# A depthwise 7x7 convolution as band products: blocks of four rows by 32 columns in place of two rows by 64

## The chip, the cores and the metric

The kernel runs on one core of a Trainium2 chip. The metric is the device time of one execution in microseconds. The engines are PE (TensorE, matrix products; PEld is its weight load), DVE (VectorE), ACT (ScalarE), POOL (GpSimd) and SP (SyncE, which only issues transfers here). All transfers of the core are carried by the same 16 DMA engines.

## The reference

Four layers act on x, eight images of 56 x 56 pixels and 192 channels in fp32. Each takes a group normalisation of x, computes something, and adds it to x. Layer 0 is a Toeplitz mixing network, layer 1 windowed attention, layer 2 a projection with a 3x3 depthwise convolution, running averages in four directions and a second projection. The change is in layer 3:

```python
x = x + _L3_conv_ref(_gn(x), ...)
# in _L3_conv_ref:
y = lax.conv_general_dilated(x, dw_kernel, window_strides=(1, 1), padding='SAME',
                             feature_group_count=c, ...) + dw_bias   # 7x7, each channel alone
y = (y - mu) * lax.rsqrt(var + EPS) * ln_gamma + ln_beta             # over the 192 channels
y = gelu(y @ w0 + b0)                                                # 192 -> 768
return (y @ w1 + b1) * gamma                                         # 768 -> 192
```

## The kernel before

**Layout.** Most of the kernel holds channels on partitions: 64 channels at a time for the upper and lower half of an image, thus 128 partitions, and three such thirds. For the depthwise convolution of layer 3 this is turned round: pixels lie on partitions and channels on the free axis, so that a 7x7 filter of one channel is a product with a band matrix.

**Preparing the images (`layer3_in`, L1190).** It runs image by image inside the loop of layer 2's output, as a generator that is advanced between the steps of that loop. It takes the group statistics, scales the image into `zp` (L1207, POOL; rows padded to 64 columns, one row of zeros above and below), and for each third of the channels turns pairs of rows into columns: 15 transposes on PE into `zps` (L1222), each 2 rows x 64 columns = 128 pixels, then copies on ACT into `zt` (L1230, and two short ones at L1233 and L1234, where the halves of the image meet). POOL fills the ends of `zt` with zeros (L1215, L1216). SP writes `zt` to the HBM buffer `zd[b]` (L1235). `NB` = 31 pairs of rows are kept per channel.

**The convolution (`convolve`, L1237).** It takes the channels in 12 groups of 16, all eight images at once. For each group SP loads the band matrices `wt` (L1250) and the images `zc` (L1253, one transfer an image), and PE computes for each channel four products into one PSUM region (L1262): `wt[:, c, q*128:(q+1)*128]` with the row pairs `q` to `q + 27` of all images, q = 0 to 3, 224 columns each. A pair of output rows needs the rows of four pairs of input rows, hence four. The band matrices are not stored: HBM holds 640 numbers a channel, and the transfer reads them with a step of one number from partition to partition, so that each partition gets 512 numbers (2 KB) a channel. DVE and ACT copy the results to `yc` (L1272, L1274), SP writes them to `yd[b]` (L1276), and POOL fetches image 0 from there at once (L1277) and adds the bias (L1286). `wt`, `zc` and `yc` have two buffers each, the PSUM tile three. SP issues in a fixed order: weights of group g+2, eight results of group g, eight images of group g+2, weights of g+3. A weight load waits until PE has ended the group whose buffer it takes. Transfers of SP share eight completion counters in turn, so each waits for the one eight places ahead: the last of the eight results waits for the weights to land, and the last of the images for the last of the results.

**After it (`layer3_norm`, L1293, and `layer3_out`).** Statistics over the channels, two per pixel pair; scaling on DVE into `yt` (L1317), transposes back on PE (L1338), and an activation with gain and shift on ACT into `y` (L1349), four pairs of rows at a time; then the two matrix products (L1361, L1372), PE's main work to the end. `layer3_norm` is a generator too, advanced inside `layer3_out`.

**The order of the work.** Within `convolve` and `layer3_in` a scheduler sets the order of instructions by its own costs, except where `manual_schedule` keeps the program's order (DVE in the loop of layer 2's output; PE, ACT and DVE in the last loop).

Of the kernel before, what the change touches and what calls it, by code (L numbers as in the profile page):

```python
# [45 lines left out]


NPAIR = H // 2
NB = NPAIR + 3
WS = 64  # L50
QR = 56 * 64
OP = 2 * WS
BAND = 4 * OP
BL = BAND + OP
CG = 16

P2 = NPAIR + 1
# [34 lines left out]
def kernel(ctx: ExitStack, tc: tile.TileContext, a: dict, out: bass.AP):  # L92
# [107 lines left out]
    def ln_var(st, nch, pool):  # L200


        P, _, n, _ = st.shape
        new = lambda name: pool.tile([P, 2, PH], F32, name=name)[:, :, 0:n]

        mean, d, var = new("ln_mean"), new("ln_d"), new("ln_var")
        nc.vector.tensor_tensor(mean, st[:, :, :, 1], st[:, :, :, 4], ALU.add)
        nc.vector.tensor_tensor(d, st[:, :, :, 1], st[:, :, :, 4], ALU.subtract)
        nc.vector.tensor_tensor(d, d, d, ALU.mult)
        nc.vector.tensor_tensor(var, st[:, :, :, 2], st[:, :, :, 5], ALU.add)  # L210
        nc.vector.tensor_scalar(var, var, 1.0 / nch, None, ALU.mult)
        nc.vector.scalar_tensor_tensor(var, d, 0.25, var, ALU.mult, ALU.add)
        return mean, var

    def ln_rows(mean, var, eps, pool):

        P, _, n = var.shape
        new = lambda name: pool.tile([P, 2, PH], F32, name=name)[:, :, 0:n]
# [4 lines left out]
        return rs, mr  # L223

    def in_halves(st):
        return st.rearrange("p (s n) k -> p s n k", s=2)
# [960 lines left out]
        nc.vector.scalar_tensor_tensor(xs, ps[:, 0:nt], vec("b_out", j), xs, ALU.add, ALU.add)  # L1187


    def layer3_in(b, x, zp, pool, psum):  # L1190
# [12 lines left out]
        yield  # L1203
        run(finish)

        for j in range(3):
            nc.gpsimd.tensor_scalar(  # L1207
                zp[:, j, 1:H // 2 + 1, 0:W], x[:, j].rearrange("p (h w) -> p h w", w=W),
                sc, sh, ALU.mult, ALU.add,
            )  # L1210
        yield

        for j in range(3):
            zt = pool.tile([OP, 64, NB], F32, name="zt")
            nc.gpsimd.memset(zt[:, :, 0:1], 0.0)  # L1215
            nc.gpsimd.memset(zt[:, :, NB - 1:NB], 0.0)  # L1216
            for m0 in range(0, PH + 1, 4):
                yield
                tp = psum.tile([OP, 4, 2, 64], F32, name="zps")
                nm = min(4, PH + 1 - m0)  # L1220
                for i in range(nm):
                    nc.tensor.transpose(  # L1222
                        tp[:, i].rearrange("p s c -> p (s c)"),
                        zp[:, j, 2 * (m0 + i):2 * (m0 + i) + 2].rearrange("p h w -> p (h w)"), ident,
                    )

                n2 = min(nm, PH - m0)
                dst = zt[:, :, 1 + m0:1 + m0 + n2]
                dst = bass.AP(dst.tensor, dst.offset, [list(dst.ap[0]), [1, n2], [PH, 2], [NB, 64]])
                nc.scalar.copy(dst, tp[:, 0:n2])  # L1230
                if nm > n2:

                    nc.scalar.copy(zt[:, :, 1 + 2 * PH], tp[:, n2, 1])  # L1233
                    nc.scalar.copy(zt[0:64, :, 1 + PH], tp[0:64, n2, 0])  # L1234
            nc.sync.dma_start(zd[b][:, 64 * j:64 * j + 64], zt)  # L1235

    def convolve(first, dwb):  # L1237
# [3 lines left out]
        with ExitStack() as st:  # L1241
            pool = st.enter_context(tc.tile_pool(reuse_waits="tile", name="cv", bufs=2))
            psum = st.enter_context(tc.tile_pool(reuse_waits="tile", name="cvp", bufs=3, space=PSUM))
            for g in range(C // CG):
                cs = slice(g * CG, g * CG + CG)
                wt = pool.tile([OP, CG, BAND], F32, name="wt")
                src = bass.AP(band.tensor, band.offset + g * CG * BL, [[1, OP], [BL, CG], [1, BAND]])

                n, queues = (CG, (nc.sync,)) if g else (4, (nc.sync, nc.gpsimd, nc.scalar))
                nc.sync.dma_start(wt[:, 0:n], src[:, 0:n])  # L1250
# [6 lines left out]
                for c4 in range(0, CG, 4):  # L1257
                    ps = psum.tile([OP, 2, 512], F32, name="cps")
                    for i in range(4):
                        dst = ps[:, i // 2, 256 * (i % 2):256 * (i % 2) + nimg * NPAIR]  # L1260
                        for q in range(4):
                            nc.tensor.matmul(  # L1262
                                dst.rearrange("p (b n) -> p b n", n=NPAIR),
                                wt[:, c4 + i, q * OP:(q + 1) * OP], zc[:, :, c4 + i, q:q + NPAIR],
                                start=(q == 0), stop=(q == 3),
                            )
# [26 lines left out]
    def layer3_norm(yl, pool, psum, dwb):  # L1293
# [7 lines left out]
        if not first:  # L1301
            for n in range(0, NPAIR, 7):
                add_bias(yl[:, :, n:n + 7], dwb)
            for k in range(5):
                yield
                ln_pieces(st, yl, range(NPAIR * k // 5, NPAIR * (k + 1) // 5))
            rows = ln_var(in_halves(st), C, pool)
            yield
            rs, mr = ln_rows(*rows, eps6, pool)

        def scaled(i0):

            yt = pool.tile([OP, 4, 3, 2, 64], F32, name="yt3")
            for i in range(min(4, PH - i0)):
                for s in range(2):
                    k = i if first else i0 + i
                    nc.vector.tensor_scalar(  # L1317
                        yt[:, i, :, s], yl[:, :, PH * s + i0 + i].rearrange("p (j c) -> p j c", j=3),
                        rs[:, s, k:k + 1], mr[:, s, k:k + 1], ALU.mult, ALU.add,
                    )  # L1320
            return yt

        ready = None
        for i0 in range(0, PH + 4, 4):
            yield
            if i0 < PH:
                if first:
                    ns = slice(i0, min(i0 + 4, PH))
                    ln_pieces(st, yl, [PH * s + n for s in range(2) for n in range(ns.start, ns.stop)])
                    rs, mr = ln_rows(*ln_var(in_halves(st)[:, :, ns], C, pool), eps6, pool)  # L1330
                following = scaled(i0)
            if ready is not None:
                i1 = i0 - 4
                ni = min(4, PH - i1)
                for j in range(3):
                    tp = psum.tile([128, 4, OP], F32, name="tp3")
                    for i in range(ni):
                        nc.tensor.transpose(  # L1338
                            tp[:, i], ready[:, i, j].rearrange("p s c -> p (s c)"), ident[0:OP, 0:OP]
                        )  # L1340

                    src = tp[:, 0:ni].rearrange("p i (s w) -> p i s w", s=2)
                    dims = [list(z) for z in src.ap]
                    src = bass.AP(
                        src.tensor, src.offset + OP - 1,
                        [dims[0], dims[1], [-dims[2][0], 2], [-dims[3][0], W]],
                    )
# [219 lines left out]
    with ExitStack() as st:  # L1567
# [6 lines left out]
        zp = pool.tile([128, 3, H // 2 + 2, WS], F32, name="zp", bufs=1)  # L1574
        nc.gpsimd.memset(zp, 0.0)
        x = [load_halves(pool, x2[0], "x2o")]
        if nimg > 1:
            ml.append(layer2_load(1, pool))
# [18 lines left out]
        for n in range(-1, len(groups)):  # L1597
# [26 lines left out]
            if k == 3:  # L1624
                run(steps)
                nc.sync.dma_start(xd[b], x[b])
                steps = layer3_in(b, x[b], zp, pool, psum)
        run(steps)


# [35 lines left out]
def _lay_out(inp):  # L1666
# [101 lines left out]
```

## Time and profile before

| | us |
|---|---|
| median of 3 runs (5647.63 to 5649.4) | 5648.63 |
| the profiled execution | 5648.44 |
| its span | 5646.6 |
| layer 3's convolution, first to last product | 303.3 (4449.5 to 4752.8) |
| PE busy in it | 299.6 |
| DVE, ACT, POOL busy in it | 29.4, 25.0, 16.3 |
| one image in the loop of layer 2's output | 57.9 |
| mean granted PE clock over the span | 0.961 |

Over the whole span PE is busy for 91%, DVE for 54%, ACT for 41%, POOL for 33%. These are averages over layers with different limits, so a stage has to be read by itself. In the profile, L12 is line 12 of the kernel. A row of a group gives the line, engine, operation, tiles and shapes, then the count, the busy time in us and the mean in ns, then the idle time of the engine just before those instructions and what ended it. Buffer numbers are left out of the names, so layer 2's convolution (L1088) and layer 3's (L1262) both show tiles `zc` and `wt`, at different lines; a name such as `in_band_dram` covers the band matrices of both layers.

### The profile page before, as it was taken

What the parts mean: (1) busy time and instruction counts of PE and PEld (TensorE: products, weight loads), DVE (VectorE), ACT (ScalarE), POOL (GpSimd) and SP (SyncE); (2) the same over time, 40 slices, a digit from 0 to 9 for tenths busy, and PEclk for the clock granted to TensorE, in tenths of its full rate; (3) what the DMA queues carried; (4) which work ended last, traced back from release to release, by engine and by line L of the source; (5) the groups of instructions that cost most, each with busy time, mean ns of one, the idle gap of its engine ahead of it and who ended that gap; (6) DMA issues with size and microseconds to landing.
All of it is one profiled execution on the core that took longest, in us unless ns stands there. A gap on an engine that the chain in (4) does not pass through costs nothing. (4 is left out here: it accounts for less than half of the span.)

```text
span 5646.6 us, 113339 instructions
## 1 busy us (share of the span) xinstructions
PE 5131.2 (91%) x49446; PEld 3421.6 (61%) x49446; DVE 3030.6 (54%) x4087; ACT 2287.3 (41%) x3100; POOL 1839.5 (33%) x1583
## 2 busy tenths in 40 slices
PE   7899969999999789999997989998888797999999
PEld 6798866666666445555554756775344697444444
DVE  4565534555554456556665868888787103433331
ACT  3344445555555333333331025554667201333333
POOL 5565655555555233334431023333010101101000
PEclk9999979999999889999998999999999898999999
DMA  5988996777777512223225756676677686212211
GB/s 148 235 226 227 223 299 245 272 273 272 273 273 274 151 36 80 74 73 81 75 62 144 266 213 228 231 241 190 185 205 212 247 330 257 78 59 78 80 39 26
DMA packets 556148, 1013.75 MB, mean 180 GB/s; under 512 B 256104, under 2 KB 479684, under 8 KB 528884
## 3 DMA queue, kind: packets, MB, share of 16 engines
q1 hardware_dynamic: 542896, 956.63, 52.8%
q0 software_dynamic: 8512, 40.62, 2.2%
q10 hardware_dynamic: 4244, 9.26, 0.6%
q8 instruction: 389, 6.37, 0.5%
q14 instruction: 107, 0.88, 0.0%
HBM read 676.92 MB, written 345.97 MB: 181 GB/s over the span
## 5 line engine op out<-in xcount | busy, mean ns | idle before, releaser
L460 POOL COPY lc<-lt 128x896 f32<-128x896 f32 (+1 forms) x320 | 590.3, 1854 | 542.8 <-PE op L468 506.6
L427 PE MATMUL qv<-w_qv_sb,x 64*112 64x256 f32 (+1 forms) x5376 | 685.7, 408 | 16.3 <-DVE act L433 12.4
L427 PEld LDWEIGHTS qv<-w_qv_sb,x 64*112 64x112 f32 x5376 | 600.2, 175 | 90.8 <-DVE act L433 22.6
L433 DVE TENSOR_TENSOR act<-qv,b_qv 112x640 f32<-112x640 f32 x448 | 318.8, 753 | 320.4 <-PE qv L427 245.0
L437 ACT ACTIVATE act<-act 112x640 f32<-112x640 f32 x448 | 300.6, 683 | 413.2 <-DVE act L433 402.7
L403 POOL TENSOR_TENSOR qv<-act 112x320 f32<-112x320 f32 x448 | 346.7, 798 | 288.4 <-ACT act L437 209.4
L468 PE MATMUL op<-rc,lc 128*56 128x56 f32 x9216 | 350.0, 221 | 61.5 <-POOL lc L460 33.0
L468 PEld LDWEIGHTS op<-rc,lc 128*56 128x56 f32 x9216 | 326.3, 135 | 129.5 <-POOL lc L460 56.6
L1361 PE MATMUL ph<-y,w_sb 64*128 64x392 f32 x2304 | 398.2, 498 | 6.5 <-ACT hid L1365 6.5
L1372 PE MATMUL po<-hid,w_sb 128*64 128x392 f32 x2304 | 386.3, 494 | 0.0
L1379 DVE TENSOR_TENSOR x<-x,z 128x392 f32<-128x392 f32 x96 | 69.6, 725 | 523.5 <-ACT z L1377 523.5
L1088 PE MATMUL cv<-zc,wt 128*128 128x224 f32 x1536 | 312.6, 355 | 25.3 <-DMA zc<-pd 24.6
L1088 PEld LDWEIGHTS cv<-zc,wt 128*128 128x128 f32 x1536 | 290.1, 189 | 68.8 <-issue 53.2
L877 PE MATMUL qk_ps<-xr,wg 64*96 64x392 f32 x1536 | 329.8, 531 | 1.7 <-DVE xr L824 1.7
L1361 PEld LDWEIGHTS ph<-y,w_sb 64*128 64x128 f32 x2304 | 220.2, 188 | 176.4 <-issue 26.1
L922 POOL TENSOR_TENSOR e<-e,mx 128x1176 f32<-128x1176 f32 x64 | 140.0, 2188 | 561.6 <-DVE mx L921 534.9
L478 PE MATMUL pj<-xn,w_p_sb 64*128 64x392 f32 x1536 | 288.8, 508 | 32.7 <-ACT pp L485 31.6
L1262 PE MATMUL cps<-zc,wt 128*128 128x224 f32 x1536 | 299.6, 356 | 18.0 <-DMA zc<-zd 15.9
L1103 POOL TENSOR_TENSOR rows<-rows,loc 128x896 f32<-128x896 f32 x96 | 218.8, 2279 | 274.7 <-ACT rows L1099 209.8
L1262 PEld LDWEIGHTS cps<-zc,wt 128*128 128x128 f32 x1536 | 289.6, 189 | 28.1 <-issue 20.5
L501 PE MATMUL y<-pp,w_o_sb 128*64 128x392 f32 x1536 | 301.2, 497 | 0.5 <-DVE pp L495 0.5
L460 DVE COPY rc<-rt 128x896 f32<-128x896 f32 (+1 forms) x160 | 215.3, 1346 | 150.4 <-PE op L468 96.8
(245 smaller groups left out, 8927.3 us busy)
## 6 DMA issues: line engine op xcount, KB each, us to landing
lt<-left SPq DMA_DIRECT2D x72, 1792.0 KB
rt<-right SPq DMA_DIRECT2D x72, 1792.0 KB
left<-qv SPq DMA_DIRECT2D x224, 252.0 KB
right<-qv SPq DMA_DIRECT2D x96, 504.0 KB
wt<-in_band_dram SPq DMA_DIRECT2D x23, 2048.0 KB
wt<-in_band_dram SPq DMA_DIRECT2D x11, 4096.0 KB
zc<-pd SPq DMA_DIRECT2D x187, 232.0 KB
pd<-pt SPq DMA_DIRECT2D x7, 5568.0 KB
```

The source lines that it names most:

```text
L403: nc.gpsimd.tensor_tensor(qv[:, s, s0:s1, k], *(acts[s][:, which, 0:n].rearrange("p (s d) -> p s d", d=64) for which in range(2)), ALU.mult,)
L427: nc.tensor.matmul(ps[s][:, which, 0:n], x[64 * s:64 * s + 64, j, bass.ts(i, 2 * W)], w_qv[64 * s:64 * s + 64, j, which, 64 * s0:64 * s1], ...
L433: nc.vector.tensor_tensor(acts[s][:, :, 0:n], ps[s][:, :, 0:n], b_qv[:, :, 64 * s0:64 * s1], ALU.add)
L437: nc.scalar.activation(acts[s][:, :, 0:n], acts[s][:, :, 0:n], AF.Silu)
L460: copy(c[:, 0:nu], raw.rearrange("p (w u d) -> p u d w", u=nu, d=64 // nu)[:, :, d0:d0 + 8])
L468: nc.tensor.matmul(op[64 * u:64 * u + W, i, :], lc[:, u, i], rc[:, u, i], start=True, stop=True)
L501: nc.tensor.matmul(y[64 * s:64 * s + 64], w_o[:, 2 * g + u, 64 * j:64 * j + 64], pp[:, u, s], start=(u == 0), stop=(u == 1),)
L877: nc.tensor.matmul(in_pairs(ps[s]), wg[64 * s:64 * s + 64, j, c0:c0 + HC], in_slots(xr[64 * s:64 * s + 64], (3 * g + j) * GW), start=(j == ...
L1088: nc.tensor.matmul(dst, wt[:, c4 + i, 128 * q:128 * q + 128], zc[:, :, c4 + i, q:q + NPAIR], start=(q == 0), stop=(q == 1),)
L1262: nc.tensor.matmul(dst.rearrange("p (b n) -> p b n", n=NPAIR), wt[:, c4 + i, q * OP:(q + 1) * OP], zc[:, :, c4 + i, q:q + NPAIR], start=(q ...
L1361: nc.tensor.matmul(ps[:, s, 0:TT], w0[64 * s:64 * s + 64, j, m * 128:(m + 1) * 128], y[64 * s:64 * s + 64, j, ts], start=(j == 0), stop=(j ...
L1372: nc.tensor.matmul(ps[64 * s:64 * s + 64], w1[:, m, 64 * j:64 * j + 64], hid[:, m, s], start=(m == 0), stop=(m == 5),)
```

## The change

The image of layer 3 is cut into a left half and a right half of 31 columns each (columns 0 to 30 and 25 to 55; 28 of each half's results are used), set in rows of 32. A block of pixels on the 128 partitions is then four rows by 32 columns. There are seven blocks in each half of the rows, 14 for each half of the columns, and a zero block at either end: `NB` = 32. Four output rows need the rows of three blocks, so a channel has three products, each still of 224 columns (8 images x 2 halves x 14 blocks). With only one empty column in 32, a band that is shifted from partition to partition would let the end of a row reach into the next, so HBM now holds the band matrices written out, 128 x 192 x 384 numbers (37.7 MB in place of 0.5 MB), and a partition's part of a group lies in one piece of 24 KB.

`layer3_in` scales into `zq` (both column halves, which overlap by six columns), makes 14 transposes and four copies for each third of the channels, and needs no short copies. `layer3_norm` picks 28 columns of each half out of the transposed blocks, and takes the statistics in quarters (row half x column half) in place of halves. The order of the transfers around the products stays as it was; around the transposes of `layer3_in` the scheduler places some transposes and copies differently.

```diff
-NB = NPAIR + 3
-WS = 64
+NQUAD = H // 4
+NB = 2 * (NQUAD + 2)
-OP = 2 * WS
-BAND = 4 * OP
-BL = BAND + OP
+QW = 32
+OP = 4 * QW
...
         for j in range(3):
+            xj = x[:, j]
             nc.gpsimd.tensor_scalar(
-                zp[:, j, 1:H // 2 + 1, 0:W], x[:, j].rearrange("p (h w) -> p h w", w=W),
+                zq[:, j, :, :, 0:QW - 1],
+                bass.AP(xj.tensor, xj.offset, [list(xj.ap[0]), [W - QW + 1, 2], [W, H // 2], [1, QW - 1]]),
                 sc, sh, ALU.mult, ALU.add,
             )
...
             zt = pool.tile([OP, 64, NB], F32, name="zt")
-            nc.gpsimd.memset(zt[:, :, 0:1], 0.0)
-            nc.gpsimd.memset(zt[:, :, NB - 1:NB], 0.0)
-            for m0 in range(0, PH + 1, 4):
-                yield
-                tp = psum.tile([OP, 4, 2, 64], F32, name="zps")
-                nm = min(4, PH + 1 - m0)
-                for i in range(nm):
-                    nc.tensor.transpose(
-                        tp[:, i].rearrange("p s c -> p (s c)"),
-                        zp[:, j, 2 * (m0 + i):2 * (m0 + i) + 2].rearrange("p h w -> p (h w)"), ident,
-                    )
-                n2 = min(nm, PH - m0)
-                dst = zt[:, :, 1 + m0:1 + m0 + n2]
-                dst = bass.AP(dst.tensor, dst.offset, [list(dst.ap[0]), [1, n2], [PH, 2], [NB, 64]])
-                nc.scalar.copy(dst, tp[:, 0:n2])
-                if nm > n2:
-                    nc.scalar.copy(zt[:, :, 1 + 2 * PH], tp[:, n2, 1])
-                    nc.scalar.copy(zt[0:64, :, 1 + PH], tp[0:64, n2, 0])
+            ends = zt.rearrange("p c (h n) -> p c h n", h=2)
+            for n in (0, NQUAD + 1):
+                nc.gpsimd.memset(ends[:, :, :, n], 0.0)
+            for h in range(2):
+                for m0, nm in ((0, 4), (4, 3)):
+                    yield
+                    tp = psum.tile([OP, 4, 2, 64], F32, name="zps")
+                    for i in range(nm):
+                        nc.tensor.transpose(
+                            tp[:, i].rearrange("p s c -> p (s c)"),
+                            zq[:, j, h, 4 * (m0 + i):4 * (m0 + i) + 4].rearrange("p r w -> p (r w)"), ident,
+                        )
+                    dst = ends[:, :, h, 1 + m0:1 + m0 + nm]
+                    dst = bass.AP(dst.tensor, dst.offset, [list(dst.ap[0]), [1, nm], [NQUAD // 2, 2], [NB, 64]])
+                    nc.scalar.copy(dst, tp[:, 0:nm])
             nc.sync.dma_start(zd[b][:, 64 * j:64 * j + 64], zt)
...
-                wt = pool.tile([OP, CG, BAND], F32, name="wt")
-                src = bass.AP(band.tensor, band.offset + g * CG * BL, [[1, OP], [BL, CG], [1, BAND]])
+                wt = pool.tile([OP, CG, 3 * OP], F32, name="wt")
+                src = band[:, cs]
...
-                        for q in range(4):
+                        z = zc[:, :, c4 + i].rearrange("p b (h n) -> p b h n", h=2)
+                        for q in range(3):
                             nc.tensor.matmul(
-                                dst.rearrange("p (b n) -> p b n", n=NPAIR),
-                                wt[:, c4 + i, q * OP:(q + 1) * OP], zc[:, :, c4 + i, q:q + NPAIR],
-                                start=(q == 0), stop=(q == 3),
+                                dst.rearrange("p (b h n) -> p b h n", h=2, n=NQUAD),
+                                wt[:, c4 + i, q * OP:(q + 1) * OP], z[:, :, :, q:q + NQUAD],
+                                start=(q == 0), stop=(q == 2),
                             )
...
-                    src = tp[:, 0:ni].rearrange("p i (s w) -> p i s w", s=2)
-                    dims = [list(z) for z in src.ap]
-                    src = bass.AP(
-                        src.tensor, src.offset + OP - 1,
-                        [dims[0], dims[1], [-dims[2][0], 2], [-dims[3][0], W]],
-                    )
-                    dst = y[:, j, 2 * W * i1:2 * W * (i1 + ni)].rearrange("p (i s w) -> p i s w", s=2, w=W)
+                    part = list(tp.ap[0])
+                    src = bass.AP(tp.tensor, tp.offset, [part, [ni * OP + QW - W // 2 - 1, 2], [QW, 4 * ni], [1, W // 2]])
+                    dst = y[:, j, 4 * W * i1:4 * W * (i1 + ni)].rearrange("p (r h w) -> p h r w", h=2, w=W // 2)
                     nc.scalar.activation(dst, src, AF.Identity, bias=vec("be3", j), scale=vec("g3", j))
...
-    band = np.zeros((C, BL), np.float32)
-    for i in range(7):
-        band[:, 124 + WS * i:131 + WS * i] = l3("dw_kernel")[i, :, 0].T
+    band = np.zeros((4, QW, C, 3, 4, QW), np.float32)
+    for q, r, p, m, dx in np.ndindex(3, 4, 4, QW - 1, 7):
+        dy, c = 4 * (q - 1) + p - r + 3, m + dx - 3
+        if 0 <= dy < 7 and 0 <= c < QW - 1:
+            band[p, c, :, q, r, m] = l3("dw_kernel")[dy, dx, 0]
+    band = band.reshape(OP, C, 3 * OP)
```

More of the change, by code (lines that the diff above doesn't have):

```diff
@@ L200, in ln_var @@
     def ln_var(st, nch, pool):
-        P, _, n, _ = st.shape
-        new = lambda name: pool.tile([P, 2, PH], F32, name=name)[:, :, 0:n]
+        P, A, n, _ = st.shape
+        new = lambda name: pool.tile([P, A, NPAIR // A], F32, name=name)[:, :, 0:n]
         mean, d, var = new("ln_mean"), new("ln_d"), new("ln_var")
@@ L215, in ln_rows @@
     def ln_rows(mean, var, eps, pool):
-        P, _, n = var.shape
-        new = lambda name: pool.tile([P, 2, PH], F32, name=name)[:, :, 0:n]
+        P, A, n = var.shape
+        new = lambda name: pool.tile([P, A, NPAIR // A], F32, name=name)[:, :, 0:n]
         rs, mr = new("ln_rs"), new("ln_mr")
@@ L223, in ln_rows, with in_quarters @@
         return rs, mr
+    def in_quarters(st):
+        return st.rearrange("p (k n) e -> p k n e", k=4)
     def in_halves(st):
@@ L1187, in layer2_out, with layer3_in @@
         nc.vector.scalar_tensor_tensor(xs, ps[:, 0:nt], vec("b_out", j), xs, ALU.add, ALU.add)
-    def layer3_in(b, x, zp, pool, psum):
+    def layer3_in(b, x, zq, pool, psum):
         sc = pool.tile([128, 1], F32, name="sc3")
@@ L1306, in layer3_norm @@
                 ln_pieces(st, yl, range(NPAIR * k // 5, NPAIR * (k + 1) // 5))
-            rows = ln_var(in_halves(st), C, pool)
+            rows = ln_var(in_quarters(st), C, pool)
             yield
             rs, mr = ln_rows(*rows, eps6, pool)
+        NQ = NQUAD // 2
         def scaled(i0):
             yt = pool.tile([OP, 4, 3, 2, 64], F32, name="yt3")
[L1314 to L1319, printed above, removed]
-                    )
+            ni = min(2, NQ - i0)
+            for h, i, s in np.ndindex(2, ni, 2):
+                k = i if first else i0 + i
+                nc.vector.tensor_scalar(
+                    yt[:, ni * h + i, :, s], yl[:, :, NQUAD * h + NQ * s + i0 + i].rearrange("p (j c) -> p j c", j=3),
+                    rs[:, 2 * h + s, k:k + 1], mr[:, 2 * h + s, k:k + 1], ALU.mult, ALU.add,
+                )
             return yt
         ready = None
-        for i0 in range(0, PH + 4, 4):
+        for i0 in range(0, NQ + 2, 2):
             yield
-            if i0 < PH:
+            if i0 < NQ:
                 if first:
-                    ns = slice(i0, min(i0 + 4, PH))
-                    ln_pieces(st, yl, [PH * s + n for s in range(2) for n in range(ns.start, ns.stop)])
-                    rs, mr = ln_rows(*ln_var(in_halves(st)[:, :, ns], C, pool), eps6, pool)
+                    ns = slice(i0, min(i0 + 2, NQ))
+                    ln_pieces(st, yl, [NQ * k + n for k in range(4) for n in range(ns.start, ns.stop)])
+                    rs, mr = ln_rows(*ln_var(in_quarters(st)[:, :, ns], C, pool), eps6, pool)
                 following = scaled(i0)
             if ready is not None:
-                i1 = i0 - 4
-                ni = min(4, PH - i1)
+                i1 = i0 - 2
+                ni = min(2, NQ - i1)
                 for j in range(3):
                     tp = psum.tile([128, 4, OP], F32, name="tp3")
-                    for i in range(ni):
+                    for i in range(2 * ni):
                         nc.tensor.transpose(
@@ L1340, in layer3_norm @@
                         )
-                    src = tp[:, 0:ni].rearrange("p i (s w) -> p i s w", s=2)
-                    dims = [list(z) for z in src.ap]
-                    src = bass.AP(
-                        src.tensor, src.offset + OP - 1,
-                        [dims[0], dims[1], [-dims[2][0], 2], [-dims[3][0], W]],
-                    )
-                    dst = y[:, j, 2 * W * i1:2 * W * (i1 + ni)].rearrange("p (i s w) -> p i s w", s=2, w=W)
+                    part = list(tp.ap[0])
+                    src = bass.AP(tp.tensor, tp.offset, [part, [ni * OP + QW - W // 2 - 1, 2], [QW, 4 * ni], [1, W // 2]])
+                    dst = y[:, j, 4 * W * i1:4 * W * (i1 + ni)].rearrange("p (r h w) -> p h r w", h=2, w=W // 2)
                     nc.scalar.activation(dst, src, AF.Identity, bias=vec("be3", j), scale=vec("g3", j))
@@ L1573 @@
         w_out = resident("w_out", nc.gpsimd, pool)
-        zp = pool.tile([128, 3, H // 2 + 2, WS], F32, name="zp", bufs=1)
-        nc.gpsimd.memset(zp, 0.0)
+        zq = pool.tile([128, 3, 2, H // 2, QW], F32, name="zq", bufs=1)
+        nc.gpsimd.memset(zq, 0.0)
         x = [load_halves(pool, x2[0], "x2o")]
@@ L1626 @@
                 nc.sync.dma_start(xd[b], x[b])
-                steps = layer3_in(b, x[b], zp, pool, psum)
+                steps = layer3_in(b, x[b], zq, pool, psum)
         run(steps)
```

## The prediction

> **What bounds the kernel now.** I began with the page's list of costly groups, which gives the convolution's row, and then followed the chain that ended last through the stage that the change touches.
>
> ```profile
> L1262 PE MATMUL cps<-zc,wt 128*128 128x224 f32 x1536 | 299.6, 356 | 18.0 <-DMA zc<-zd 15.9
> L1262 PEld LDWEIGHTS cps<-zc,wt 128*128 128x128 f32 x1536 | 289.6, 189 | 28.1 <-issue 20.5
> ```
>
> The 192 channels with four band products each are 768 products, and each leaves two records (fp32), so a group of 16 channels is 128 records. They fill 299.6 us, and of the 18.0 us of idleness before them 15.9 are waits for images, 14.3 of that ahead of the first product.
>
> ```profile
> 4439.51 9.88 DMA zc<-zd
> 4449.39 0.14 issue
> 4449.52 76.31 PE cps L1262 x384
> ...
> 4601.17 14.64 DMA wt<-in_band_dram
> 4615.82 4.58 DMA yd<-yc
> 4620.42 5.69 DMA zc<-zd
> 4626.11 0.35 issue
> 4626.46 24.89 PE cps L1262 x128
> ```
>
> In this chain of work (start, length, what) a group of 128 records takes 24.89 us on PE. The middle lines are the lesson: 4601.17 to 4626.11, the transfers of one group, one behind the other, take 24.94 us. PE and transfers are level. The stages show how much slack the transfers have (columns: window, its length, busy PE, PEld, DVE, ACT, POOL, then granted clock, DMA share, GB/s):
>
> ```profile
> 4449.50:4752.80 303.30, 299.56 (x1536) 289.57 (x1536) 29.37 (x47) 25.02 (x47) 16.31 (x22) 0.99 0.85 310
> 4449.50:4454.00 4.50, 4.48 (x12) 4.08 (x13) 0.00 (x0) 0.00 (x0) 0.00 (x0) 0.51 1.05 396
> 4552.00:4574.00 22.00, 22.00 (x116) 21.48 (x116) 1.88 (x3) 1.64 (x4) 1.48 (x2) 1.00 1.02 375
> 4574.00:4577.00 3.00, 2.19 (x12) 1.83 (x11) 0.62 (x1) 0.53 (x1) 0.00 (x0) 1.00 0.08 29
> 4588.00:4598.50 10.50, 10.50 (x57) 10.26 (x56) 1.25 (x2) 1.06 (x2) 1.48 (x2) 1.00 1.04 395
> 4764.00:4782.00 18.00, 2.84 (x9) 1.59 (x10) 16.65 (x35) 1.39 (x4) 10.33 (x4) 0.50 1.00 428
> ```
>
> The DMA engines are full for 22 us of each group, then empty for 3 us until PE frees a weight buffer. So the stage is PE's, by 3 us in 25. It is 303.3 us = 12 x 24.89 (298.7) + 2.25 (the first 4.5 us run at half clock) + 2.3 of small waits. SP's own waits say the same from the other side:
>
> ```profile
> SPq L1250 <- PE cps L1262: 53.9, 10, 7.0
> SPq L1276 <- DMA wt<-in_band_dram: 51.7, 10, 6.1
> ```
>
> The weight load of a group (L1250) waits for PE; the last write of results (L1276) waits until that load has landed, and the image loads (L1253) stand behind it on SP.
>
> **What the Trainium skill says.** DMA: Bandwidth & Descriptors, "Latency and other measured facts", lists rates that fall when rows of different partitions lie large powers of two apart in HBM (512 KiB still 207 of 214 GB/s, 4 MiB 103). The new band rows lie 192 x 384 x 4 B = 288 KiB apart; no run here shows such a pitch, but rows of 9 to 21 KB (yl, x, w0) move at 428 GB/s in the last window above. SBUF — State Buffer, "Door 1: The DMA port swizzle", says that SBUF works in 16-byte lines and that at least two hits per line are needed for full rate. TensorE: Matmul & The Clock Gate, "What's actually happening", puts the return to half clock after some 3.4 us of idleness; the trace agrees on the half clock after the long wait (0.51), and shows 1.00 through short ones.
>
> **The change part by part.** All sums are made against the profiled execution, 5648.44 us (span 5646.6 and 1.8 around it); the median of the runs is 5648.63, the same.
>
> *The products.* Three bands of 224 columns replace four. A record costs 24.89/128 = 194.5 ns; 96 make 18.67 us a group, 6.22 less. The moving operand is now 16 runs of 14 elements for 8 of 28. A matmul on 392 columns in one run (L1361) takes 12.05 us per 72 records on half the rows, two side by side, 334.7 ns a pair or 0.854 ns a column; here it is 0.868 with 28-runs, so run length hardly shows. The new runs begin at 64-byte steps plus 0, 4 or 8 bytes, so every line that is read is hit at least twice. I take no extra; the bounds are 0 and 10% (the trace has no row with such short runs to read it from), and nothing suggests a gain.
>
> *The transfers.* A group moved 4.194 MB of weights (2 KB rows), 2.032 of image, 1.835 of results and 0.229 of image 0 again: 8.29 MB in 22.0 us. Now the weights are 3.146 MB in rows of 24 KB, the image 2.097. At 395 GB/s (the window of 2 KB rows) the weights took 10.6 us; at 415, between that and 428, they take 7.6; at 395 again 8.0. The image adds 0.2. So the engines are full for 22.0 - 3.0 + 0.2 = 19.2 us: more than PE's 18.67. The bound changes hands.
>
> *The period.* SP's order is unchanged: weights of g+2, eight results of g, eight images of g+2, and a weight load still waits for PE to end g. From that issue to PE's start on g+2 is D: 1.5 us to the first byte (issue 4575.49, full from 4577), 19.2, and about 1.2 to the semaphore (4598.6 to about 4599.8): 21.9 us. Two buffers give a period of (21.9 + 18.67)/2 = 20.3, if each load starts on an empty queue; 19.2 if they run back to back. Neither holds fully, since the load is now issued as the last image transfer lands: I take 20.0. PE then idles 1.3 us a group, too short for half clock.
>
> *The stage.* Group 0: 18.67 + 2.25 for the clock. Group 1: 18.67, its data being some 5 us earlier than before (in time by 4472.5 then, less 2.1 MB). Ten groups at 20.0. Sum 239.6 against 303.3: **-63.7 us**.
>
> *Preparing the image (layer3_in).* Per channel third, 15 transposes and six ScalarE copies become 14 and four:
>
> ```profile
> L1230 ACT COPY zt<-zps x96: 609/1096/1188, 4043.5 to 4435.3; 128x512 f32<-128x512 f32 x72, 128x256 f32<-128x256 f32 x24
> L1233 ACT COPY zt<-zps x24: 319/336/390, 4048.3 to 4435.8; 128x64 f32<-128x64 f32 x24
> L1234 ACT COPY zt<-zps x24: 312/327/387, 4048.4 to 4435.9; 64x64 f32<-64x64 f32 x24
> ```
>
> Before: 3 x 1.096 + 0.65 + 0.34 + 0.33 = 4.6 us. After: two of 512 and two of 384 (by the slope between 256 and 512, 0.87): 3.9. That is 2.0 us of ACT per image, and 0.4 of PE. One image takes 57.9 us here, with PE 51.3, DVE 45.0 and ACT 39.9 busy, so none is full; copies to zt hold 1.6% of the chain from 3908 us on, some 28 us over the eight images, of which 15% are 4. I take **-3** (bounds 0 and -16: all of it hidden, or all of it seen). The copies write at 128-byte steps instead of 124: one hit per line both ways, so no change; a conflict at that step would cost up to as much again per copy, some 25 us in all, mostly under PE. GpSimd's scaling grows from 1568 to 1736 elements (1.65 to 1.83 us), hidden by the 29.5 us that GpSimd waits before it; on the last image 0.2 is seen. Its zero fills become fewer and wider, under waits for zd. The reordering of single transposes on PE and ACT that follows goes with the same bounds.
>
> *The start of the convolution.* SP sends the first weights only behind the last image's third zd write; three thirds at 0.66 bring that 2.0 us forward, and 0.26 MB less stand ahead of the first images (0.8 us at 336 GB/s): **-2.5**.
>
> *After the convolution.* Results to yl, statistics, the load of w0 and PE's first product take 30 us, with the same instructions: 0. In layer3_norm normalisations, transposes and activations keep their numbers and sizes (14 transposes per third and 448 elements, now in runs of 28 read forwards instead of 56 backwards), beneath a PE that is full in chunks of 12.0 us: 0. Layers 0 to 2 don't change.
>
> Sum: -63.7 - 3 - 2.5 = -69.2, so **5579 us**.
>
> **The rivals.** *PE stays the bound.* If the long rows reach 428 GB/s and D overlaps well, the period is PE's 18.7: 12 x 18.67 + 2.25 = 226.3, -77.0, and with the rest 5566. For it: full load time and PE time differ by half a microsecond. Against: the SP chain, in which the results' eighth write waits for the weights.
>
> *The transfers lose more.* A dip to 268 GB/s stands in the trace where weights end and results begin (4561 to 4563); if the shorter cycle has two such dips, or the weights come at 300 GB/s (10.5 us, +2.9), or matmuls on 14-runs cost 10% (20.5 us), the period is 21 to 22.5: ten groups times +1 to +2.5, 5589 to 5604.
>
> *The weights come slowly: slower than before.* The old source was 0.5 MB in all, read over and over; the new one is 37.7 MB, each byte read once, 128 rows 288 KiB apart. If HBM serves that badly, the loop is DMA's. The gain is gone when the stage takes 303.3 + 5.5: (308.8 - 39.6)/10 = 26.9 us a group, thus 15.3 for the weights, 205 GB/s. At 180 it is 17.5, period 29.1, 5670. Against it: yl, x and w0 are also read once, at 428 GB/s.
>
> *It does nothing* would need PE to have had slack, which 24.89 us against 22 of transfers excludes.
>
> **How the numbers follow.** Transfers pace at about 20: 0.58 (own range 5570 to 5590). PE paces: 0.21. Transfers lose more: 0.15. Slow weights: 0.05, nearly all slower. The last 0.01 lies between. Within 0.2% (11 us, about what a measurement of this kernel can tell from no change) is 0.01, faster 0.94, slower 0.05. The range 5559 to 5606 takes in the first three cases.
>
> **What would show it.** The row of the products has 1152 records in 12 groups of 18.7 us; the stage lasts about 240 us at a DMA share near 0.95; the chain passes from PE to wt, yd and zc in most groups, not three times. PE's wait for zc grows to some 13 us besides the first. The zt copies fall to 96 in all. Wrong would be: a product over 200 ns, weights that take longer than 10 us from issue, or zt copies over 1.2 us.

## The result: 1% faster, with 12 us of the stage's gain missing

The changed kernel takes 5589.33 us in the median of four runs (5583.77 to 5597.44), the kernel before 5649.01 in the same comparison: a ratio of 0.9895, 95% interval 0.9878 to 0.9912. The profiled execution took 5588.73 us (span 5586.9), 59.7 less than the one before. The forecast was 5579.0.

Where the 59.7 us are, between the two profiled executions (the first row is read from the start of the last product into `mx`, layer 2's running averages):

| stretch | before | after | change | forecast |
|---|---|---|---|---|
| last `mx` product to the first product of the convolution | 521.2 | 512.0 | -9.2 | -5.5 |
| the same, as a place in the span (the layers ahead ended 2.0 later) | 4449.5 | 4442.3 | -7.2 | -5.5 |
| the convolution, first to last product | 303.3 | 251.4 | -51.9 | -63.7 |
| its end to the first product with w0 (L1361, now L1359) | 30.1 | 30.2 | +0.1 | 0 |
| from there to the end | 863.7 | 863.0 | -0.7 | 0 |

The miss is in the convolution; the stretch ahead of it gained a little more than forecast. Its groups of costly instructions after the change (busy us, mean ns | idle before, and what ended it):

```profile
L1262 PE MATMUL cps<-zc,wt 128*128 128x224 f32 x1152 | 232.6, 366 | 31.0 <-DMA zc<-zd 31.0
L1262 PEld LDWEIGHTS cps<-zc,wt 128*128 128x128 f32 x1152 | 228.0, 199 | 35.5 <-issue 32.8
```

PE's idle time has risen from 18.0 us to 31.0, and now all of it waits for images: 12.2 ahead of the first product, 18.8 between groups. PE's part of the timeline of the kernel after (start, length, what, the idle time before it) shows where these 18.8 us stand:

```profile
4442.33 37.94 PE L1262 MATMUL cps<-zc,wt 128*128 128x224 f32 x192 [12.22 <-DMA zc<-zd]
4483.70 39.42 PE L1262 MATMUL cps<-zc,wt 128*128 128x224 f32 x192 [3.43 <-DMA zc<-zd]
4527.37 38.09 PE L1262 MATMUL cps<-zc,wt 128*128 128x224 f32 x192 [4.25 <-DMA zc<-zd]
4569.19 39.35 PE L1262 MATMUL cps<-zc,wt 128*128 128x224 f32 x192 [3.73 <-DMA zc<-zd]
4612.43 38.22 PE L1262 MATMUL cps<-zc,wt 128*128 128x224 f32 x192 [3.89 <-DMA zc<-zd]
4654.10 39.55 PE L1262 MATMUL cps<-zc,wt 128*128 128x224 f32 x192 [3.45 <-DMA zc<-zd]
```

Each row is 192 records, two groups of 96. Groups go in pairs: the second follows the first without a gap, then PE waits 3.4 to 4.3 us. From 4483.70 to 4654.10 there are four pairs, 42.6 us each, thus 21.3 a group. I had taken 20.0.

The loop that makes the pair can be read from the transfers that SP issues (time of issue, length, what):

```profile
4504.99 0.33 SPq L1249 DMA_DIRECT2D wt<-in_band_dram  x1
...
4523.15 0.33 SPq L1249 DMA_DIRECT2D wt<-in_band_dram  x1
4524.38 11.16 SPq L1276 DMA_DIRECT2D yd<-yc  x8
4535.85 4.33 SPq L1252 DMA_DIRECT2D zc<-zd  x8
4547.33 0.33 SPq L1249 DMA_DIRECT2D wt<-in_band_dram  x1
```

The load of 4504.99 feeds the group that PE starts at 4527.37: 22.4 us. Its next free weight buffer comes when PE has ended that group, at 4547.31, and the next such load goes out at 4547.33. A pair is therefore one load's latency plus one group of products. Between the load of 4504.99 and that of 4523.15 lie 18.16 us, which is 96 records of 189.2 ns: that is a group at full speed. And the windows of one pair (window, length, busy PE, PEld, DVE, ACT, POOL, granted clock, DMA share, GB/s) show what both sides do meanwhile:

```profile
4506.50:4544.00 37.50, 33.25 (x168) 32.62 (x168) 4.37 (x7) 3.72 (x7) 2.96 (x4) 0.95 1.00 377
4544.00:4548.50 4.50, 4.50 (x26) 4.50 (x25) 0.62 (x1) 0.51 (x1) 0.00 (x0) 1.00 0.33 91
4527.00:4531.00 4.00, 3.63 (x11) 3.38 (x12) 0.00 (x0) 0.00 (x0) 0.00 (x0) 0.57 1.02 424
4442.30:4693.70 251.40, 232.58 (x1152) 227.96 (x1152) 29.37 (x48) 25.01 (x47) 16.27 (x22) 0.94 0.87 328
```

The first two rows are the pair: the DMA engines carry two groups in one stretch of 37.5 us and then nearly stand still for 4.5, until a buffer is free. The third row is the start of a pair on PE: PE stands still once in a pair too, and when it begins again its clock is at 0.57. The fourth is the whole stage. So neither is the bound: PE's 18.16 us a group and the transfers' 18.75 (37.5/2) would both allow a shorter period than 21.3. What bounds, on this reading, is that each waits for the other over two buffers; the experiments test it.

In the chain that ended last (start, length, what) the time goes from one to the other in every pair; the product rows here are single groups, and the three shown, each right after a wait, take 19.9 to 21.3 us, not 18.16:

```profile
4483.70 21.28 PE cps L1262 x96
...
4508.62 11.63 DMA yd<-yc
...
4521.33 5.74 DMA zc<-zd
4527.37 19.94 PE cps L1262 x96
...
4551.47 11.14 DMA yd<-yc
4563.00 5.74 DMA zc<-zd
4569.19 21.20 PE cps L1262 x96
```

### The profile page after: what moved, and what is told of

The parts are those of the page before. It is cut to its first block, busy times and chain, and to the rows that moved or that the text cites. A ratio compares the mean times of both kernels' runs of the same rounds, so it can differ in the third digit from the quotient of the medians.

```text
span 5586.9 us, 112500 instructions
## 1 busy us (share of the span) xinstructions
PE 5053.5 (90%) x49038; PEld 3368.0 (60%) x49038; DVE 3034.3 (54%) x4087; ACT 2278.7 (41%) x3052; POOL 1845.9 (33%) x1583
## 5 line engine op out<-in xcount | busy, mean ns | idle before, releaser
L429 PEld LDWEIGHTS qv<-w_qv_sb,x 64*112 64x112 f32 x5376 | 616.0, 175 | 71.8 <-DVE act L435 20.0
L1359 PE MATMUL ph<-y,w_sb 64*128 64x392 f32 x2304 | 397.9, 498 | 6.5 <-ACT hid L1363 6.5
L1359 PEld LDWEIGHTS ph<-y,w_sb 64*128 64x128 f32 x2304 | 220.2, 188 | 176.1 <-issue 25.6
L1370 PEld LDWEIGHTS po<-hid,w_sb 128*64 128x64 f32 x2304 | 162.7, 137 | 213.8 <-issue 213.8
L497 DVE TENSOR_TENSOR pp<-pp,ot 128x784 f32<-128x784 f32 x128 | 124.3, 971 | 300.9 <-PE ot L492 253.6
```

The lines of the kernel that those rows point to most:

```text
L429: nc.tensor.matmul(ps[s][:, which, 0:n], x[64 * s:64 * s + 64, j, bass.ts(i, 2 * W)], w_qv[64 * s:64 * s + 64, j, which, 64 * s0:64 * s1], ...
L1359: nc.tensor.matmul(ps[:, s, 0:TT], w0[64 * s:64 * s + 64, j, m * 128:(m + 1) * 128], y[64 * s:64 * s + 64, j, ts], start=(j == 0), stop=(j ...
L1370: nc.tensor.matmul(ps[64 * s:64 * s + 64], w1[:, m, 64 * j:64 * j + 64], hid[:, m, s], start=(m == 0), stop=(m == 5),)
```

## The experiments

**The theory**: two buffers close a loop, load latency plus one group in each pair. **Its rivals**: the transfers are full or slow (their bytes, the rows' place in HBM, the order on SP), or PE has become slower (short runs, half clock).

Where an experiment's stage is read from a window, the window ends with the start of the last record, 0.35 us before that record's end. The last four experiments have one execution each, while the kernel after alone ranges from 5583.77 to 5597.44: only their traces are compared, not their times.

**A third buffer** for weights and images, in the kernel after. It moves no byte less and leaves every product as it was.

```diff
-                wt = pool.tile([OP, CG, 3 * OP], F32, name="wt")
+                wt = pool.tile([OP, CG, 3 * OP], F32, name="wt", bufs=3)
...
-                zc = pool.tile([OP, nimg, CG, NB], F32, name="zc")
+                zc = pool.tile([OP, nimg, CG, NB], F32, name="zc", bufs=3)
```

> The changed kernel with three buffers for the weights and the images instead of two. Theory (the two buffers make a loop of one load and one group of products, 22.2 + 18.2 us per two groups, plus the half clock after each wait): the loads start before PE frees a buffer, the period falls from 21.3 to that of the transfers, some 19.4 us; the convolution takes some 235 us instead of 251.4, no group waits for more than 1.5 us, and the clock stays at 1.00; some 5573 us in all. Rival (the DMA engines' rate sets the period of 21.3): the convolution stays at 251.

Measured: 5560.89 us (5558.94 to 5569.94), ratio to the kernel before 0.9845 (0.983 to 0.9859). The timeline of PE and the window of the stage:

```profile
4440.54 93.88 PE L1262 MATMUL cps<-zc,wt 128*128 128x224 f32 x480 [12.76 <-DMA zc<-zd]
4534.85 127.72 PE L1262 MATMUL cps<-zc,wt 128*128 128x224 f32 x672 [0.43 <-issue]
```

```profile
4440.50:4662.20 221.70, 221.23 (x1151) 219.69 (x1152) 29.35 (x47) 25.03 (x47) 16.29 (x22) 0.99 0.96 371
```

The stage falls from 251.4 to 221.7 us, and PE runs through it with one gap of 0.43: 127.72/672 = 190 ns a record, 18.2 us a group. PE is now the bound. The theory holds, and the gain is larger than I expected, since the transfers have no floor at 19.2: 7.3 MB go by for each 18.2 us of PE. The 371 GB/s are the mean of the stage, part of whose loads lie ahead of it; in its middle, 4480 to 4625 us, the DMA engines move 396 GB/s at a share of 1.03. So the transfers have no slack to be seen either: the two are level. This version beats both kernels.

**The third buffer for the weights alone**, to see which of the two closed the loop.

```diff
-                wt = pool.tile([OP, CG, 3 * OP], F32, name="wt")
+                wt = pool.tile([OP, CG, 3 * OP], F32, name="wt", bufs=3)
```

> The kernel after with three buffers for the weights alone; the images keep two. Loop of two buffers through the weights: it is the weight load that SP cannot issue until PE ends a group, and the images of g+2 stand behind the results of g anyway, so the second buffer of the images costs nothing. Then the stage lasts about 222 us as with three of both, the waits between groups are gone and the time is about 5561. Rival, the images' buffer closes the loop as well: an image load still waits for PE to end the group two before, the queue still runs empty once per pair, the stage stays over 235 and the time is 5574 or more.

Measured: 5565.73 us (5562.1 to 5567.62), ratio 0.9854 (0.9835 to 0.9872); the stage lasts 223.7 us, with two small gaps of 0.87 and 1.09:

```profile
4448.60 57.48 PE L1262 MATMUL cps<-zc,wt 128*128 128x224 f32 x288 [12.96 <-DMA zc<-zd]
4506.95 36.56 PE L1262 MATMUL cps<-zc,wt 128*128 128x224 f32 x192 [0.87 <-DMA zc<-zd]
4544.60 128.05 PE L1262 MATMUL cps<-zc,wt 128*128 128x224 f32 x672 [1.09 <-issue]
```

A third buffer for the weights is enough to open the loop; one more for the images is worth at most these 2 us. That the images' third buffer alone would not do it follows from the order on SP, where the weight load comes first, but was not run.

**The same edit in the kernel before**, where PE was the bound.

```diff
-                wt = pool.tile([OP, CG, BAND], F32, name="wt")
+                wt = pool.tile([OP, CG, BAND], F32, name="wt", bufs=3)
```

> The kernel before with three buffers for the weights. There PE was busy for 299.6 of the 303.3 us, so a third buffer can take away only the small waits and the half clock at the start, not PE's 24.9 us a group: the stage 299 to 303.5, the time within 5 us of the kernel before. A gain of 10 us or more would mean that the earlier start of loads is worth something by itself, and then part of what the third buffer gained after the change did not come from the loop that the change had closed.

Measured: 5646.05 us (5636.76 to 5650.65), ratio 0.9996 (0.9987 to 1.0004), no difference that can be told. The stage itself gets shorter by 5.4 us, 297.9 for 303.3 and just below the 299 to 303.5 expected; 3.6 of these are its small waits, which are gone:

```profile
4455.07 297.89 PE L1262 MATMUL cps<-zc,wt 128*128 128x224 f32 x1536 [14.91 <-DMA zc<-zd]
```

So the buffer that gains some 27 us in the stage after the change gains 5 in it before. It was the change that made the two buffers the bound.

**PE kept warm**: in the kernel after, eight products whose results nobody uses run ahead of every even group, so that PE isn't idle long enough to lose its clock. (Not shown: the zero tile `warm`, and a line that keeps PE in the program's order.)

```diff
...
+                if g >= 2 and g % 2 == 0:
+                    idle = psum.tile([OP, 512], F32, name="idle", bufs=1)
+                    for _ in range(8):
+                        nc.tensor.matmul(idle[:, 0:224], ident, warm, start=True, stop=True)
```

> The changed kernel with eight extra products of 224 columns (3.0 us) on PE ahead of every second group, where PE waits 3.4 to 4.3 us for images; their result is used by nothing. Theory (each such wait costs a further 1.7 to 3.1 us because the clock falls to half): the waiting groups take 18.2 us like the others instead of 19.9 to 21.3, the clock stays at 1.00 after the first group, the convolution takes 239 us instead of 251.4. Rival (the loop is paced by transfers, so a faster PE only waits longer): 249 to 251, or more where the extra products come at the wrong place.

Measured: 5590.87 us (5569.84 to 5596.95), ratio 0.9888 (0.9867 to 0.9909), no difference to the kernel after that can be told; the stage is 247.0. Two rows of PE's timeline and the window of the stage:

```profile
4535.77 18.38 PE L1269 MATMUL cps<-zc,wt 128*128 128x224 f32 x96
4557.42 18.40 PE L1269 MATMUL cps<-zc,wt 128*128 128x224 f32 x96 [3.27 <-issue]
```

```profile
4454.20:4701.20 247.00, 237.66 (x1231) 234.59 (x1232) 29.35 (x47) 25.03 (x47) 16.28 (x22) 0.99 0.91 334
```

The groups now take 18.3 to 18.4 us at a clock of 0.99, as was meant, except one of 20.08. But new waits of up to 3.3 us stand ahead of the odd groups, and the pairs (40.2, 42.9, 41.4, 43.5) are hardly shorter. Of the 12 us expected, 4 came. The transfers between 4515 and 4655 ran at 339 to 377 GB/s at a share of 0.93 to 1.02, while three buffers gave 371 over the whole stage. Why they were slower here stays open. Nor does the run separate the clock from the extra products themselves: the even groups start right behind them, with no wait of their own but one of 0.23 us, so their images may have landed earlier, and the 3.0 us of extra products may have held PE up. What it shows is that taking the half clock away in this manner doesn't open the loop.

**Results written from ACT's queue** instead of SP's, so that images don't stand behind them.

```diff
-                    nc.sync.dma_start(yd[b][:, cs], yc[:, b])
+                    nc.scalar.dma_start(yd[b][:, cs], yc[:, b])
```

> The changed kernel with the results' writes issued by ACT instead of SP, so that the images no longer stand behind them. Theory (a loop of latencies): from PE's freeing of a buffer to the landing of the images it takes 1.5 + 8 + 5.4 + 1.2 = 16 us plus what the results share of the engines, under PE's 18.2 or near it; the convolution takes 222 to 238 us. Rival (rate of the DMA engines): as many bytes, so 251 still. A third outcome, ACT held up by its issuing of 96 transfers (0.4 us each, 38 us), would show as PE waiting for ACT.

Measured: 5607.23 us (5591.65 to 5617.12), ratio 0.9921 (0.9902 to 0.994). The stage takes 251.8 with the same pairs. The edit did not do what it was meant to, as SP's waits in the stage show:

```profile
SPq L1252 <- DMA yd<-yc: 132.5, 63, 13.3
```

The images (L1252) still wait for results, though another engine issues these: in this program the eight completion counters are shared by the transfers of both, in turn, and in the trace each image waits for the counter that one of ACT's writes took before it. A load of weights went out at 4528.02, its group's first image at 4540.61. So this run says nothing for or against the order on SP. It loses a little elsewhere: from the last product to the first with w0 it takes 42.2 us for 30.2.

**Both**, three buffers and results from ACT:

> Both: three buffers, and the results' writes issued by ACT. Theory: nothing is left but PE's 18.2 us a group or the engines' time for 7.3 MB, 19.3 us; 222 to 235 us for the convolution, no less than the better of the two alone by more than 10. If the rate of the transfers is the floor, 232; if PE is, 221. Rival (rate of the DMA engines at 21.3): 251.

Measured: 5584.5 us (5580.48 to 5589.33), ratio 0.9881 (0.9864 to 0.9897), worse than three buffers alone; the stage lasts 235.4 us, just outside what was expected. The first 456 records, nearly five groups, run back to back, then PE waits for the copies of the results on ACT, up to 9.10 us at once:

```profile
4589.71 38.20 PE L1262 MATMUL cps<-zc,wt 128*128 128x224 f32 x192 [9.10 <-ACT yc L1274]
```

This is the third outcome named for ACT's queue above: ahead of this wait ACT spent 15.55 us (from 4573.53) on the issue of eight writes, with its copies behind them.

**Short rows of the weights**: the kernel after reads 1.5 KB rows from the first 0.5 MB of the band matrices, so it multiplies by other weights.

```diff
-                src = band[:, cs]
+                src = bass.AP(band.tensor, band.offset + g * CG * 640, [[1, OP], [640, CG], [1, 3 * OP]])
```

> The changed kernel, its weights read as rows of 1.5 KB from the first 0.5 MB of the band matrices, with a step of one number from partition to partition, in place of rows of 24 KB from 37.7 MB; the weights are then the wrong ones. Theory (length of row and place in HBM don't matter at these sizes, 393 GB/s against 395): the weights land in 9 to 11 us from their issue and the convolution takes 248 to 256 us. Rival (the long rows are worth what the prediction gave them, or HBM serves the large array badly): longer than 258 us, or shorter than 245.

Measured in one execution: 5600.06 us, the stage 253.0 with 325 GB/s against 328. The one weight load that stands in the chain of each run took 12.00 us from its issue, for 10.96 in the kernel after and 9 to 11 expected. So the long rows from the large array are not slower than short rows from a small one; they may be a little faster. Length of row and size of array were changed together, so a gain of one could hide a loss of the other. The rival of slow weights doesn't need this run: in the kernel after, rows 288 KiB apart moved at 393 GB/s where the old ones moved at 395.

**A step of 17 places in place of 16** between the halves' blocks (`NB` = 34): the 14-runs of the moving operand then begin 68 bytes apart, no longer 64.

```diff
-NB = 2 * (NQUAD + 2)
+NP = NQUAD + 3
+NB = 2 * NP
...
-            for n in (0, NQUAD + 1):
+            for n in (0, NQUAD + 1, NQUAD + 2):
```

> The changed kernel with 17 places instead of 16 per half row of blocks, so that runs of 14 start at steps of 68 bytes. Theory (alignment): a record takes 194 ns or more, up to 200, a group 18.6 to 19.2 us. Rival (only the smaller number of bytes or the new shape counts): 189.2 ns as in the changed kernel. The image transfers grow by 6%, so the convolution takes 252 to 258 us.

Measured in one execution: 5597.62 us, the stage 256.9. A group alone, without a clock loss:

```profile
4486.56 19.01 PE L1263 MATMUL cps<-zc,wt 128*128 128x224 f32 x96 [3.03 <-DMA yd<-yc]
```

Rows of 96 records that are cut in the same way took 18.3 to 18.4 us with PE kept warm, so where the runs lie costs some 3.5%. (The median distance between the starts of records is 200 ns here, 189 in the kernel after, 193 to 194 in the kernel before. The 200 hides two kinds, see below.)

**The kernel before with `NB` = 32**, so that its 28-runs begin 128 bytes apart:

```diff
-NB = NPAIR + 3
+NB = NPAIR + 4
...
-            nc.gpsimd.memset(zt[:, :, NB - 1:NB], 0.0)
+            nc.gpsimd.memset(zt[:, :, NB - 2:NB], 0.0)
```

> The kernel before with 32 places instead of 31 per channel in the image tiles, so that each run of 28 numbers starts on the same place of a 128-byte step; four products as before. Theory (a product on misaligned runs costs more, which is why a record fell from 194.5 to 189.2 ns): 189 ns a record, 24.2 us a group where nothing waits; the convolution gains little, 297 to 303 us, since the loads take 25 us a group. Rival (run length or the number of runs matters): 194.5 ns still.

Measured in one execution: 5648.98 us beside 5652.03 for the kernel before. The stage is 303.8, so the step alone does not make the stage shorter, and neither the theory nor the rival fits as a whole. Only those with q = 0, whose runs begin on the step itself, come every 188 to 189 ns; those shifted by 4, 8 or 12 bytes every 193 to 195. The 14-runs of the kernel after come at 189 whatever their shift.

One rule sorts the records of all four traces. Cut the tile, from its start in each partition, into pieces of 16 bytes and count how many of them a run touches. A 28-run (112 bytes) touches 7 if it begins on such a piece, and 8 otherwise; a 14-run (56 bytes) touches 4 if it begins 0, 4 or 8 bytes into one, and 5 at 12. Products whose runs all touch the smaller number come every 188 to 189 ns: a quarter of them in the kernel before (with steps of 124 bytes the runs of channel after channel begin elsewhere), a quarter with `NB` = 32, all of them in the kernel after, and half of them with 17 places. The rest come every 193 to 195 ns with 28-runs, and with 17 places every 200 to 204, though there only every second run touches one piece more. Why the second costs more than the first is open.

**The short copies put back** into `layer3_in` of the kernel after, two per third:

```diff
+                    if m0 and h:
+                        nc.scalar.copy(ends[:, :, 1, 7], tp[:, 2, 0])
+                        nc.scalar.copy(ends[0:64, :, 1, 14], tp[0:64, 2, 1])
```

> The changed kernel with two short copies of 64 columns put back on ACT at the end of each third of the channels (they write again what is there). Theory (ACT's copies hold the chain of layer 2's output, so 0.66 us of them less per third gave the 7.2 us by which the convolution starts earlier): the convolution starts 4 to 7 us later than the 4442.3 us of the changed kernel. Rival (the new order of transposes gave it): less than 1.5 us later.

Measured in one execution: 5592.31 us. The convolution starts at 4445.5 us, 3.2 later than in the kernel after, between the two forecasts. From the last `mx` product to the convolution it takes 517.5 us, for 512.0 without and 521.2 before; alone this would speak for ACT's copies as the cost. But the kernel before with `NB` = 32 has all its copies and takes 511.7. What both shorter ones share is ACT's wait for DVE, in the waits between 3928 and 4436 us: first the kernel after, then the kernel before with `NB` = 32, then the one with the short copies.

```profile
ACT ln_rs L219 <- DVE ln_var L211: 45.0, 11, 14.0
```

```profile
ACT ln_rs L220 <- DVE ln_var L212: 46.0, 11, 14.2
```

```profile
ACT ln_rs L219 <- DVE ln_var L211: 55.0, 11, 14.4
```

It is 54.7 us in the kernel before. What goes with it is the order in which the scheduler sets transposes and copies. In this stretch ACT's instructions of the kernel before with `NB` = 32 follow the order of the kernel after (418 of 420 match, in sequence), while those of the kernel before match in 393 only; and the kernel before with three buffers, whose order is that of the kernel before, takes 521.1 us. Putting the copies back changed the order as well (394 of 420), so it doesn't show what a copy costs. Which of the reordered instructions does it wasn't tried.

## Why the prediction was right, and where its steps failed

**D and the loop: right; "the bound changes hands": only in part.** PE is no longer the bound, but the transfers alone are not it either. The latency from a weight load's issue to PE's start was put at 21.9 us; the five loads that PE waited for took 21.6 to 22.4, 21.9 in the mean. The formula (D + group)/2 describes the stage: (21.9 + 20.6)/2 = 21.25, with 20.6 the mean of the groups right after a wait, against 21.3 measured. That the sum comes out says only that the load is issued when the group ends; that the loop is the bound is shown by the third buffer. The time is off by 10 us. The signs named for it came in part: all waits for images, but 18.8 us for 13, a share of the DMA engines of 0.87 for 0.95, and a chain that changes sides once in a pair, not in most groups.

**"I take 20.0": failed.** I had the formula's 20.3 and went below it, because loads might partly overlap. They do overlap, two by two, but then the next pair starts on an empty queue, and the formula holds in full. The step after it, "PE then idles 1.3 us a group, too short for half clock", is where the size went: the waits come bunched, 3.4 to 4.3 us in every second group, and the group after takes 20.6 us for 18.16. The two groups ahead of the loop took 37.9 for the 39.6 forecast; the ten others 21.3 for 20.0, +13.4. Together +11.8, which is the miss of the stage. Going below the formula itself cost little: with the product at its real 18.16 us it gives (21.9 + 18.16)/2 = 20.0, the very value taken, by two errors that cancel. It is the 2.4 us of half clock in every pair, 1.2 a group, that carry it from 20.0 to 21.3. The Trainium skill, which I named for this (TensorE: Matmul & The Clock Gate, "What's actually happening": half clock after some 3.4 us of idleness), agrees in the kernel after, where every wait of 3.43 us and more is followed by it (0.57 in the window above). It isn't sharp: with PE kept warm, a wait of 3.27 us cost no clock, and one of 2.22 us was followed by two microseconds at a clock of 0.50 and the group of 20.08.

**The product's price, 194.5 ns with "nothing suggests a gain": mis-sized.** It is 189.2 ns, 18.16 us a group for 18.67. About 1 ns of this is the way of reading: 24.89 us counts the end of a group's last record, which the next group overlaps, and start to start the old records lie 193 to 194 ns apart. (For the same reason the sum 12 x 24.89 + 2.25 left only 2.3 us for small waits, where PE's timeline of the kernel before has 0.81, 0.68, 0.91 and 1.22, thus 3.6.) The rest goes with where the runs lie. The argument from lines that are hit at least twice (SBUF — State Buffer, "Door 1: The DMA port swizzle") doesn't reach: with `NB` = 32 in the kernel before, products shifted by 8 bytes read 28-runs, which touch no line only once, and still came every 193 ns; what counts in these traces is whether a run touches a line more than its length needs.

**The transfers: 19.2 us a group: a little too much, without effect on the time.** The whole of two groups went by in 37.5 us, thus 18.75 a group; with three buffers 18.2 were enough. The 415 GB/s for the weights was about right: a window of 4 us in the first load of a pair has 393, windows of 4 us in the second 406 to 455. One sign of being wrong did come, weights that take longer than 10 us from issue: the load at 4632.52 took 10.96. It was set too tight, since the prediction's own terms, 1.5 + 7.6 + 1.2, already give 10.3.

**Before the convolution: the sign was right, the reason was not shown.** -7.2 or -9.2 us for the -5.5 forecast. The copies shrank about as worked out: 107.4 us in all to 93.3, 1.8 an image for the 2.0 forecast, with 0.885 us for the form of 384 columns (0.87 by the slope). But the step that turned them into time, "copies to zt hold 1.6% of the chain", falls with the run that keeps all copies and is as early. That the sum of -5.5 came near was luck.

**After it: right**, +0.1 and -0.7 us for 0.

**The rivals.** "The transfers lose more" gave 5589 to 5604 and a period of 21 to 22.5; time and period are met, its mechanism isn't: the dips of the DMA rate stay at one a group (58 GB/s at 4514, 257 at 4533), the weights aren't slow, the product isn't dearer. "PE stays the bound" named the state that comes with the third buffer (221.7 us at 189 to 190 ns), not this one. Slow weights are excluded. The range held the time, and the 5589 lies inside the middle case's own 5570 to 5590, but barely and with luck: the half clock that the prediction left out is partly made good by the cheaper product and the earlier start, of which it had forecast neither the size nor the reason.

## What to carry to other kernels

When two stages of a pipeline come level, neither rate tells the period: work out the loop, (latency from a load's issue to its use + time of one use)/number of buffers, and put a buffer more where it exceeds both rates. Here the one edit `bufs=3` on the weights is worth some 23 us after the change (ratio 0.9854 for 0.9895) and nothing before it. Don't shade such a sum downward for overlap: here what overlapped in one round was paid in the next, and the waits bunched until they cost the clock as well.

## What I had not expected of the hardware

Where the runs of a moving operand lie changes a record of 224 fp32 columns: 188 to 189 ns where no run touches more pieces of 16 bytes than its length needs (14-runs that begin 0, 4 or 8 bytes into one, 28-runs that begin on one), 193 to 195 for the other 28-runs, and 200 to 204 where every second 14-run begins 12 bytes into a piece. In this program transfers from SP and from ACT share completion counters, so moving the writes to ACT left SP's loads waiting for them, 132.5 us in the stage. And reads and writes together held 371 GB/s over 222 us, 396 in the middle, while PE waited once, for 0.43 us.
